# Idle accumulator banks for the gates, relu fused into the residual, fewer masks in the chains, squares on ScalarE: a graph network on one core

## The chip, the core and the metric

The kernel runs on one core of a Trainium2 chip. The metric is device time in microseconds of one execution. The kernel before takes 737.91 us, the median of three runs (737.57 to 739.96); the execution in its profile spans 734.9 us. PE, DVE, ACT, POOL and SP below are TensorE, VectorE, ScalarE, GpSimd and SyncE, as in the profile.

## The reference

x has 3327 nodes with 64 features, adj is 3327 x 3327, sparse in content (about one entry in 200 is not zero) but stored dense. Four layers follow each other, each with a layernorm ahead of it; the sums with x are the residuals.

```python
h = relu(layernorm(x))            # layer 0: two gated convolutions
for W, wih, whh in layer0:
    m = adj @ (h @ W)
    r, z, n = gru_gates(m @ wih.T, h @ whh.T)
    h = relu((1 - z) * n + z * h)
x = x + h

h = relu(layernorm(x))            # layer 1: the ranked layer
mask = adj != 0
rank = cumsum(mask, axis=1); deg = rank[:, -1:]
k = minimum(deg, 100); pos = rank - (deg - k)
w = mask * where(pos > 0, 0.5 ** (k - pos), 0)
x = x + w @ (h @ W) + b

h = relu(layernorm(x))            # layer 2: three hops
for W, b in layer2:
    h = ((adj * adj) @ h) @ W.T + b
x = x + h

g = h = relu(layernorm(x))        # layer 3: two hops
for W in layer3:
    h = tanh(concat([adj @ h, h], 1) @ W)
x = x + h
```

## The kernel before, in words

**Passes and chunks.** Eight times adj is multiplied with features: passes k = 0 and 1 for layer 0, k = 2 for the ranked layer, 3 to 5 for the squared hops, 6 and 7 for the last two (KIND, line 70). The destination nodes lie in four chunks of 384, 384, 384 and 512 columns, twice over (two halves s; CH, line 51), and the chunks in two groups, 0 and 1, 2 and 3 (GROUPS). adj [...]is streamed from memory in every pass: 26 tiles of 128 source nodes for each group, each 128 x 2 x 768 or 896 numbers of 32 bits (load, L325), into 20 slots. `alone` and `joint` (L555 to L620) write out the order of the units (pass, chunk, tile), such that a tile once loaded serves two passes; `run` (L622) loads 60 units ahead, prepares up to 44 units ahead, and expands EXPAND = 3 units ahead of the matmuls of `propagate` (L517), which sum into a PSUM bank per chunk.

**The engines' order** is the order in which this program issues the instructions; nothing rearranges it later. Each engine takes its own in that order.

**Chains.** When a chunk's sum is complete, a chain of work begins (`after_0` to `after_7`), for the chunk's new features: a gated cell (`gru`, L737: evacuation of the sum L704 and L705, four gates L748, sigmoids L753, DVE work L757 to L768, relu L773 in the second cell), transposes (through `mm`, L229), the residual (L728), a layernorm (L713 to L724, of which L720, a power, runs on GpSimd), and for the ranked layer the features as a sum of three bf16 terms (`in_three`, L791 and L793). A chain is a generator; each `yield` gives microseconds of PE work after which it may go on, and `spend` (L294) lets chains go on as matmuls are issued. A unit that needs features which a chain has not yet made runs this chain to its end (L508).

**Banks.** [...]four for sums of `propagate`, four for everything else. `take` (L238) gives an idle one; with either=True, which only the ranked weights use, it may also be an idle bank of the sums.

**The ranked pass.** w isn't computed from a cumulative sum along all columns, but by tiles: a mask of each tile (adj != 0, bf16, two `piece`s of L383 on DVE), whose last row is filled by a DMA of GpSimd (L388) with the number of entries in later tiles (counted by L453 during pass 0). A matmul with a triangular matrix (`tri`, through `mm`, L229) gives the exponents, and an eviction with a relu turns them into int16, which is the bit pattern of the bf16 weight (`e`): L431 on DVE or L433 on ACT, by the rule in L430. `propagate` multiplies e with the three terms of the features. Pieces wait in a queue (`pieces`); L645 to L648 issue some of them per unit, and `mask_pieces(t=t)` (L424) issues what is still missing of a tile when the tile is expanded. A tile is called "own" of a group where its sources lie among the group's destinations. In group 0 the own tiles come last in pass 2, right after group 0's chains of pass 1, so DVE and ACT do chains and weights there at the same time.

**The rest of what is touched.** `square` (L358) squares a tile of adj for the squared passes, two of three on ACT (L360), one of three on DVE (L362). `last_sources` (L469) fetches the last row of every tile for a group and makes its weights (L481, L485, L487); it is begun at 70 us of PE work for group 0, 230 for group 1 (L914).

The lines below are those of the kernel before.

Of the kernel before, what the change touches and what calls it, by code (L numbers as in the profile page):

```python
# [12 lines left out]
AF = mybir.ActivationFunctionType  # L13
ALU = mybir.AluOpType
# [37 lines left out]
NC = len(CH)  # L52
CWM = 512
GROUPS = [(0, 1), (2, 3)]
# [39 lines left out]
def kernel(  # L94
# [9 lines left out]
    nc = tc.nc  # L104
# [116 lines left out]
    def width(c):  # L221
        return blocks(c) * P
# [12 lines left out]

    released = [0] * 8

    def take(sums=False, either=False):  # L238

        pool = idle_sums if sums else idle_temps  # L240
        if either and idle_sums and (not pool or released[idle_sums[0]] < released[pool[0]]):
            pool = idle_sums
        for c in list(tasks):
            if not pool and c not in running:
                advance(c)
        i = pool.popleft()
        return i, banks[i]
# [9 lines left out]
    def flat(t):  # L257
        return t.rearrange("p b s d -> p b (s d)")
# [4 lines left out]
    def xchunk(c):  # L263
        return xs[:, CH[c][0]:CH[c][1]]
# [5 lines left out]
    tasks = {}  # L270
# [10 lines left out]
    def begin(c, task):  # L281
        finish(c)
        tasks[c] = [task, 0.0]
        advance(c)

    def finish(c):
        while c in tasks:
            advance(c)

    def later_task(us, task):  # L290
        yield us
        yield from task
# [12 lines left out]
    sums = {}  # L305
# [50 lines left out]
                spare.append(self.at)  # L356

    def square(sq, v, turn):  # L358
        if turn % 3:
            nc.scalar.activation(sq, v, AF.Square)  # L360
        else:
            nc.vector.tensor_tensor(sq, v, v, ALU.mult)  # L362
# [31 lines left out]
    def mask_pieces(n=0, t=None):  # L394

        while pieces and (n > 0 or any(u is t for u, _, _ in pieces)):
            _, half, piece = pieces.popleft()
            piece(half)
            n -= 1

    def expand(k, c, t):

        if k == COUNT:
            return None
        w = width(c)
        if t is SPECIAL:
            g = c // 2
            w0 = (CH[c][0] - CH[GROUPS[g][0]][0]) * P
            finish(NC + 1 + g)
            return lastw[g][:, w0:w0 + w].bitcast(BF16)  # L410
        if KIND[k] == PLAIN or (KIND[k] == SQUARED and t.in_place):
            return t.view(c)
        if KIND[k] == SQUARED:
            room = Mask(t.w)
            wide = room.view.rearrange("p s w -> p (s w)").bitcast(F32)[:, :2 * w].rearrange("p (s w) -> p s w", s=2)
            square(wide, t.view(c), t.q + c)
            squared[k, c, t] = room
            return wide
        wide = work.tile([P, 2, CWM], I16, name="e", bufs=4)[:, :, :w]

        mask_pieces(t=t)  # L424
        for s in range(2):
            i, ps = take(either=True)
            mm(ps[:, :w], tri, t.mask.view[:, s, t.cols(c)])
            own = chunk_of(t.q % NB) in GROUPS[t.g]
            busy = any((k - 1, ch) in sums for ch in GROUPS[t.g])
            if s and (own if t.g == 0 and (own or busy) else c == GROUPS[t.g][1]):  # L430
                nc.vector.tensor_scalar(wide[:, s], ps[:, :w], BITS, 0.0, op0=ALU.add, op1=ALU.max)  # L431
            else:
                nc.scalar.activation(wide[:, s], ps[:, :w], AF.Relu, bias=bitsb)  # L433
            give(i)
        spend(STREAM_US * w / CWM * 0.5)
        if c == GROUPS[t.g][1]:
            t.mask.free()
        return wide.bitcast(BF16)

    ranks_left = set(sources_of(*GROUPS[0]))  # L440
    counts = {}
    squared = {}

    def count(t, first, last):


        mask_pieces(t=t)
        for c in GROUPS[t.g]:
            w = width(c)
            if first:  # L450
                counts[c] = take()
            for s in range(2):
                nc.tensor.matmul(counts[c][1][s * D:(s + 1) * D, :w], behind[:, NQ - 1 - t.q:NQ - 1 - t.q + D],  # L453
                                 t.mask.view[:, s, t.cols(c)], start=first, stop=last)
            spend(STREAM_US * w / CWM * 0.25)
            if last:
                begin(("count", c), count_done(c))
        t.mask.free()
# [163 lines left out]
    def run():  # L622
        total = {}
        for k, c, t in units:
            total[k, c] = total.get((k, c), 0) + 1
        done = {}
        loaded, prepared, expanded = 0, 0, deque()
        for i, (k, c, t) in enumerate(units):
            while loaded < len(units) and loaded < i + LOAD:
                u = units[loaded][2]  # L630
                if u is not SPECIAL and u.slot is None:
                    if len(dead) <= RESERVE and loaded > i + EXPAND:
                        break
                    u.load()
                loaded += 1
            while prepared < loaded and prepared < i + PREPARE[KIND[units[prepared][0]] if units[prepared][0] != COUNT
                                                               else COUNT]:
                if prepared > i + PREPARE[PLAIN] and not spare and len(dead) <= RESERVE + 1:
                    break
                prepare(*units[prepared])  # L640
                prepared += 1
            while len(expanded) < min(EXPAND + 1, len(units) - i):
                assert prepared > i + len(expanded)
                expanded.append(expand(*units[i + len(expanded)]))
            if k != 2:  # L645
                mask_pieces(1 + len(pieces) // 6)
            elif not (c in GROUPS[0] and (t is SPECIAL or chunk_of(t.q % NB) in GROUPS[0])):
                mask_pieces(1)  # L648
            n = done[k, c] = done.get((k, c), 0) + 1
            propagate(k, c, t, expanded.popleft(), n == 1, n == total[k, c])  # L650

# [72 lines left out]
        nc.vector.scalar_tensor_tensor(groups(h), xc[:, :n], 0.0, st[:, 3, :n, None].to_broadcast([P, n, D]),  # L724
                                       op0=ALU.max, op1=ALU.mult)

    def residual(v, c):
        nc.vector.tensor_tensor(flat(xchunk(c)), flat(xchunk(c)), v[1], ALU.add)  # L728
        give(v[0])

    def add_row(c, i):
# [5 lines left out]
    def gru(acc, c, bi, bh, cell, pace=1.0):  # L737

        w = width(c)
        evacuate_stacked(acc, c)  # L740
        yield 0.8 * pace
        at = dead.popleft()
        r, z, d = (slots[at].rearrange("p s w -> p (s w)")[:, i * CWM:i * CWM + w] for i in range(3))

        def gate(g):
            i, ps = take()
            for s in range(2):
                nc.tensor.matmul(ps[upper(1 - s), :w], cells[:, cell, s, g, :], both[c][:, s], start=True, stop=True)  # L748
            return i, ps

        for g, v in enumerate((r, z)):
            i, ps = gate(g)
            nc.scalar.activation(v, ps[:, :w], AF.Sigmoid, bias=bsum[:, cell, g:g + 1])  # L753
            give(i)
        pn = gate(2), gate(3)
        yield 1.0 * pace
        nc.vector.scalar_tensor_tensor(r, pn[0][1][:, :w], bcol[:, bh + 2:bh + 3], r, op0=ALU.add, op1=ALU.mult)  # L757
        nc.vector.tensor_tensor(r, r, pn[1][1][:, :w], ALU.add)
        for i, _ in pn:
            give(i)  # L760
        yield 1.0 * pace
        nc.scalar.activation(r, r, AF.Tanh, bias=bcol[:, bi + 2:bi + 3])
        yield 0.8 * pace
        for s in range(2):
            u = upper(1 - s)
            nc.vector.tensor_tensor(d[u], both[c][u, s], r[u], ALU.subtract)
        nc.vector.tensor_tensor(d, d, z, ALU.mult)
        nc.vector.tensor_tensor(d, d, r, ALU.add)  # L768
        if cell == 0:
            nc.scalar.activation(both[c][upper(1), 0], d[upper(1)], AF.Relu)  # L770
            nc.vector.tensor_scalar(both[c][upper(0), 1], d[upper(0)], 0.0, None, op0=ALU.max)
        else:
            nc.scalar.activation(d, d, AF.Relu)  # L773
        yield 2.8 * pace
        return at, d

# [43 lines left out]
    def after_1(c, acc):  # L820
        pace = 1.0 if c in GROUPS[0] else 1.2
        at, h2T = yield from gru(acc, c, BI2, BH2, 1, pace)
        v = transpose_to_nodes(h2T, c)
        dead.append(at)
        yield 0.8 * pace
        residual(v, c)
        yk = nodes(c)
        yield from layernorm_relu(yk, c, TWO27, 1.2 * pace)
        y[2][c] = yield from in_three(yk, c)
        yield 6.0  # L830
        add_row(c, 3)
# [79 lines left out]
            begin(c, before_0(c))  # L911
    begin(NC, more_constants())
    begin(NC + 1, later_task(70.0, last_sources(0)))
    begin(NC + 2, later_task(230.0, last_sources(1)))  # L914
    run()
    for c in list(tasks):
        finish(c)
# [39 lines left out]
```

## Time and profile before

| what | value |
| --- | --- |
| median of three runs | 737.91 us |
| profiled span | 734.9 us |
| sums of the plain and squared passes, PE L517 f32 | 536.0 us busy, 2912 records |
| sums of the ranked pass, PE L517 bf16 | 72.9 us, 624 records |
| masks by tri, PE L229 bf16 (temp and sum banks) | 67.0 us, 416 records |
| mask pieces, DVE L383 | 112.5 us, 208 instructions |
| squares, ACT L360 and DVE L362 | 113.7 us in 138, 69.4 us in 70 |
| evictions to e from temp banks, ACT L433 and DVE L431 | 68.8 us in 123, 23.5 us in 37 |
| evictions to e from sum banks, ACT L433 and DVE L431 | 13.6 us in 24, 13.7 us in 24 |
| rows of totals, issued by POOL (L388) | 52 |
| power of the layernorm, POOL L720 | 27.0 us in 16 |
| relu of the second cell, ACT L773 | 2.2 us in 4 |

A row of the page gives line, engine, operation, output and inputs by their names in the program, the count, the busy time and the mean of one. "Idle before" is how long the engine stood ahead of such an instruction, and behind the arrow is what ended that. In the timelines of a single engine, a row is a run of like instructions from its start, with its length, and in brackets the idle time ahead of it. In a table of stretches each engine has its busy time and its count, in the order PE, weight load, DVE, ACT, POOL; then come the clock granted to PE and the share and rate of the DMA.

### The profile page before, as it was taken

Reading aid. Unit: us, or ns where it says so; the run is one execution under the profiler, and the core shown is the slowest. Engines: PE = TensorE matmul, PEld = TensorE weight load, DVE = VectorE, ACT = ScalarE, POOL = GpSimd, SP = SyncE. Lnnn points to the kernel's source line nnn. Section 1 sums busy time; section 2 is a strip of 40 time slices with the busy share of each in tenths; the row PEclk is TensorE's granted clock in tenths of the full one; section 3 lists DMA queues with packets and bytes.
Section 4 is the critical chain, followed back from the end, with each engine's and each line's share of the span. In section 5 each row is a group of like instructions: output and inputs, shape, how many; then the busy total and the mean of one; then the engine's idle time right before and its main releaser. Section 6 shows DMA issues by size and latency. Waiting matters only on the chain. (4 is left out here: it accounts for less than half of the span.)

```text
span 734.9 us, 12499 instructions
## 1 busy us (share of the span) xinstructions
PE 694.7 (95%) x5112; PEld 347.6 (47%) x5112; DVE 340.1 (46%) x599; ACT 244.6 (33%) x383; POOL 72.6 (10%) x105
## 2 busy tenths in 40 slices
PE   5988999899999898989899999999999999999997
PEld 2543566344546685545344444334344454344443
DVE  6656736434997978758764114321252520000101
ACT  0103100212037767768848213730044601000101
POOL 4100000001290502112200000000110000000000
PEclk9999999999999999999999999999999999999999
DMA  9999996189587365571799749953987399916991
GB/s 340 401 357 405 405 392 213 44 323 364 179 288 280 105 219 186 183 283 45 276 351 383 263 145 408 406 230 109 393 298 251 126 396 405 401 39 238 399 403 38
DMA packets 68964, 201.54 MB, mean 274 GB/s; under 512 B 7388, under 2 KB 8644, under 8 KB 68908
## 3 DMA queue, kind: packets, MB, share of 16 engines
q1 hardware_dynamic: 66156, 199.70, 73.2%
q8 instruction: 40, 0.66, 0.4%
q10 hardware_dynamic: 576, 0.85, 0.3%
q0 software_dynamic: 2176, 0.20, 0.2%
q14 instruction: 16, 0.13, 0.0%
HBM read 199.68 MB, written 0.85 MB: 273 GB/s over the span
## 5 line engine op out<-in xcount | busy, mean ns | idle before, releaser
L517 PE MATMUL sum<-adj,y 128*64 128x384 f32 (+1 forms) x2912 | 536.0, 516 | 17.8 <-DMA adj<-in_adjT 13.5
L517 PEld LDWEIGHTS sum<-adj,y 128*64 128x64 f32 x2912 | 218.4, 138 | 274.0 <-issue 230.3
L360 ACT ACTIVATE adj<-adj 128x768 f32<-128x768 f32 (+1 forms) x138 | 113.7, 891 | 57.7 <-PE sum L517 36.6
L383 DVE TENSOR_SCALAR adj<-adj 128x768 bf16<-128x768 f32 (+3 forms) x208 | 112.5, 593 | 33.5 <-PE temp L453 29.5
L362 DVE TENSOR_TENSOR adj<-adj 128x768 f32<-128x768 f32 (+1 forms) x70 | 69.4, 1022 | 57.1 <-DMA adj<-in_adjT 32.6
L433 ACT ACTIVATE e<-temp,bitsb 128x384 int16<-128x384 f32 (+1 forms) x123 | 68.8, 600 | 24.2 <-PE temp L229 18.4
L517 PE MATMUL sum<-e,adj 128*64 128x384 bf16 (+1 forms) x624 | 72.9, 339 | 0.0
L705 DVE COPY both<-sum 64x384 f32<-64x384 f32 (+1 forms) x16 | 9.5, 594 | 130.5 <-ACT both L704 130.5
L704 ACT COPY both<-sum 64x384 f32<-64x384 f32 (+1 forms) x16 | 8.0, 499 | 149.4 <-PE sum L517 149.4
L229 PE MATMUL temp<-adj,tri 128*64 128x384 bf16 (+1 forms) x320 | 49.6, 346 | 7.9 <-DMA adj<-totals 2.5
L720 POOL TENSOR_TENSOR st<-st,mhalf 128x6 f32<-128x6 f32 (+1 forms) x16 | 27.0, 1688 | 301.1 <-DVE st L719 292.6
L517 PEld LDWEIGHTS <-adj 128*64 128x64 bf16 x624 | 41.3, 110 | 17.2 <-issue 5.3
L388 POOL DMA_DIRECT2D adj<-totals x52 | 31.4, 606 | 134.6 <-DVE adj L768 74.7
L229 PEld LDWEIGHTS <-tri 128*64 128x64 bf16 x416 | 28.6, 111 | 29.2 <-issue 14.7
L431 DVE TENSOR_SCALAR e<-temp 128x512 int16<-128x512 f32 (+1 forms) x37 | 23.5, 634 | 20.5 <-PE temp L229 11.4
L748 PE MATMUL temp<-both,cells 128*64 128x384 f32 (+1 forms) x128 | 27.4, 521 | 4.1 <-DVE adj L757 2.2
L658 DVE COPY t<-sum 128x384 f32<-128x384 f32 x8 | 4.4, 556 | 54.3 <-PE sum L517 54.3
L453 PE MATMUL temp<-adj,behind 128*64 128x384 bf16 x208 | 28.6, 339 | 0.3 <-DVE adj L383 0.2
L656 ACT COPY t<-sum 128x384 f32<-128x384 f32 (+1 forms) x8 | 4.3, 533 | 67.0 <-PE sum L517 67.0
L700 ACT COPY both<-temp 64x384 f32<-64x384 f32 (+1 forms) x16 | 8.0, 502 | 55.5 <-PE temp L694 55.4
L453 PEld LDWEIGHTS <-behind 128*64 128x64 bf16 x208 | 16.2, 110 | 16.2 <-issue 14.4
L229 PE MATMUL sum<-adj,tri 128*64 128x384 bf16 (+1 forms) x96 | 17.4, 335 | 2.4 <-DVE e L431 2.4
(83 smaller groups left out, 293.5 us busy)
## 6 DMA issues: line engine op xcount, KB each, us to landing
adj<-in_adjT SPq DMA_DIRECT2D x130, 768.0 KB, 7.7
adj<-in_adjT SPq DMA_DIRECT2D x104, 896.0 KB, 11.6
xs<-in_x SPq DMA_DIRECT2D x1, 640.0 KB
out<-xs ACTq DMA_DIRECT2D x3, 192.0 KB, 1.9
adj<-totals POOLq DMA_DIRECT2D x26, 3.0 KB, 4.6
adj<-totals POOLq DMA_DIRECT2D x26, 3.5 KB, 2.2
folds<-in_weights SPq DMA_DIRECT2D x4, 64.0 KB, 11.8
out<-xs ACTq DMA_DIRECT2D x1, 256.0 KB
```

The source lines that it names most:

```text
L229: nc.tensor.matmul(out[hs], lhsT[:, hs], rhs, start=start, stop=stop)
L360: nc.scalar.activation(sq, v, AF.Square)
L362: nc.vector.tensor_tensor(sq, v, v, ALU.mult)
L383: nc.vector.tensor_scalar(t.mask.view[:rows, half], t.view()[:rows, half], 0.0, None, op0=ALU.not_equal)
L388: nc.gpsimd.dma_start(out=t.mask.view[P - 1:P], in_=totals[t.g][t.q:t.q + D + 1:D, :])
L431: nc.vector.tensor_scalar(wide[:, s], ps[:, :w], BITS, 0.0, op0=ALU.add, op1=ALU.max)
L433: nc.scalar.activation(wide[:, s], ps[:, :w], AF.Relu, bias=bitsb)
L453: nc.tensor.matmul(counts[c][1][s * D:(s + 1) * D, :w], behind[:, NQ - 1 - t.q:NQ - 1 - t.q + D], t.mask.view[:, s, t.cols(c)], start=firs ...
L517: nc.tensor.matmul(acc[h * D:(h + 1) * D, :w], yq[h], rhs[h], start=first and n == 0, stop=last and n == len(terms) - 1)
L705: nc.vector.tensor_copy(both[c][upper(1), 1], acc[1][upper(1), :width(c)])
L720: nc.gpsimd.tensor_tensor(st[:, 3, :n], st[:, 2, :n], mhalf[:, :n], ALU.pow)
L748: nc.tensor.matmul(ps[upper(1 - s), :w], cells[:, cell, s, g, :], both[c][:, s], start=True, stop=True)
```

## The change

Gates, transposes and the other temporary results may take an idle bank of the sums (`take`, either=True by default), except for the counts. The relu after the second cell is no instruction of its own any more: the residual takes max(v, 0) and adds in one DVE instruction. In pass 2 the mask pieces that were issued one per unit ahead of need are no longer issued while group 0 runs and any chunk has a chain under way. While a ranked sum of group 1 is open, all squares go to ScalarE, not two of three. The rule of L430 gives the second half of a weight to DVE more often in the units that are not own. The last sources of group 1 are begun at 175 us of PE work instead of 230.

```diff
--- before.py
+++ after.py
@@ -235,8 +235,10 @@
 
     released = [0] * 8
 
-    def take(sums=False, either=False):
-
+    def take(sums=False, either=True):
+
+
+        either = either and not sums
         pool = idle_sums if sums else idle_temps
         if either and idle_sums and (not pool or released[idle_sums[0]] < released[pool[0]]):
             pool = idle_sums
@@ -356,7 +358,7 @@
                 spare.append(self.at)
 
     def square(sq, v, turn):
-        if turn % 3:
+        if turn % 3 or any((2, c) in sums for c in GROUPS[1]):
             nc.scalar.activation(sq, v, AF.Square)
         else:
             nc.vector.tensor_tensor(sq, v, v, ALU.mult)
@@ -423,11 +425,11 @@
 
         mask_pieces(t=t)
         for s in range(2):
-            i, ps = take(either=True)
+            i, ps = take()
             mm(ps[:, :w], tri, t.mask.view[:, s, t.cols(c)])
             own = chunk_of(t.q % NB) in GROUPS[t.g]
             busy = any((k - 1, ch) in sums for ch in GROUPS[t.g])
-            if s and (own if t.g == 0 and (own or busy) else c == GROUPS[t.g][1]):
+            if s and (own if t.g == 0 and (own or busy) else not own or c == GROUPS[t.g][1]):
                 nc.vector.tensor_scalar(wide[:, s], ps[:, :w], BITS, 0.0, op0=ALU.add, op1=ALU.max)
             else:
                 nc.scalar.activation(wide[:, s], ps[:, :w], AF.Relu, bias=bitsb)
@@ -448,7 +450,7 @@
         for c in GROUPS[t.g]:
             w = width(c)
             if first:
-                counts[c] = take()
+                counts[c] = take(either=False)
             for s in range(2):
                 nc.tensor.matmul(counts[c][1][s * D:(s + 1) * D, :w], behind[:, NQ - 1 - t.q:NQ - 1 - t.q + D],
                                  t.mask.view[:, s, t.cols(c)], start=first, stop=last)
@@ -645,7 +647,8 @@
             if k != 2:
                 mask_pieces(1 + len(pieces) // 6)
             elif not (c in GROUPS[0] and (t is SPECIAL or chunk_of(t.q % NB) in GROUPS[0])):
-                mask_pieces(1)
+                if c in GROUPS[1] or not any(ch in tasks for ch in range(NC)):
+                    mask_pieces(1)
             n = done[k, c] = done.get((k, c), 0) + 1
             propagate(k, c, t, expanded.popleft(), n == 1, n == total[k, c])
 
@@ -724,8 +727,11 @@
         nc.vector.scalar_tensor_tensor(groups(h), xc[:, :n], 0.0, st[:, 3, :n, None].to_broadcast([P, n, D]),
                                        op0=ALU.max, op1=ALU.mult)
 
-    def residual(v, c):
-        nc.vector.tensor_tensor(flat(xchunk(c)), flat(xchunk(c)), v[1], ALU.add)
+    def residual(v, c, relu=False):
+        if relu:
+            nc.vector.scalar_tensor_tensor(flat(xchunk(c)), v[1], 0.0, flat(xchunk(c)), op0=ALU.max, op1=ALU.add)
+        else:
+            nc.vector.tensor_tensor(flat(xchunk(c)), flat(xchunk(c)), v[1], ALU.add)
         give(v[0])
 
     def add_row(c, i):
@@ -769,8 +775,6 @@
         if cell == 0:
             nc.scalar.activation(both[c][upper(1), 0], d[upper(1)], AF.Relu)
             nc.vector.tensor_scalar(both[c][upper(0), 1], d[upper(0)], 0.0, None, op0=ALU.max)
-        else:
-            nc.scalar.activation(d, d, AF.Relu)
         yield 2.8 * pace
         return at, d
 
@@ -823,7 +827,7 @@
         v = transpose_to_nodes(h2T, c)
         dead.append(at)
         yield 0.8 * pace
-        residual(v, c)
+        residual(v, c, relu=True)
         yk = nodes(c)
         yield from layernorm_relu(yk, c, TWO27, 1.2 * pace)
         y[2][c] = yield from in_three(yk, c)
@@ -911,7 +915,7 @@
             begin(c, before_0(c))
     begin(NC, more_constants())
     begin(NC + 1, later_task(70.0, last_sources(0)))
-    begin(NC + 2, later_task(230.0, last_sources(1)))
+    begin(NC + 2, later_task(175.0, last_sources(1)))
     run()
     for c in list(tasks):
         finish(c)
```

## The prediction, on record before the changed kernel ran

> **What bounds the kernel now.** I read the page first, then PE's waits, then busy time by stretch, then the timelines around the longest waits.
>
> The page's first part:
>
> ```profile
> PE 694.7 (95%) x5112; PEld 347.6 (47%) x5112; DVE 340.1 (46%) x599; ACT 244.6 (33%) x383; POOL 72.6 (10%) x105
> ```
>
> PE is busy for 694.7 of 734.9 us. The change removes no matmul, so it can win only PE's idle time, or the part of it that other engines cause. Who caused it stands in PE's waits (total, times, longest):
>
> ```profile
> PE sum L517 <- DVE y L724: 3.1, 1, 3.1
> PE temp L229 <- DMA adj<-totals: 2.5, 1, 2.5
> PE sum L229 <- DVE e L431: 2.4, 3, 1.4
> PE temp L748 <- DVE adj L757: 2.2, 1, 2.2
> PE temp L229 <- DVE adj L383: 2.0, 3, 1.6
> PE temp L748 <- ACT both L704: 1.9, 1, 1.9
> ```
>
> The longest wait of all, 13.5 us for tiles of adj, lies mostly ahead of 60 us and is not touched. What is touched lies in the ranked phase (208 to 360 us). Busy time of PE, PEld, DVE, ACT, POOL, then clock and DMA:
>
> ```profile
> 236.00:256.00 20.00, 15.49 (x190) 12.07 (x191) 19.59 (x44) 15.02 (x31) 8.56 (x12) 1.00 0.38 126
> ...
> 272.00:292.00 20.00, 17.59 (x200) 13.38 (x198) 15.85 (x31) 13.69 (x26) 3.82 (x4) 1.00 0.65 226
> ...
> 318.00:330.00 12.00, 9.54 (x62) 4.09 (x60) 6.52 (x11) 6.49 (x10) 2.16 (x4) 0.86 0.72 273
> ...
> 346.00:361.00 15.00, 11.87 (x120) 6.62 (x118) 11.85 (x20) 11.62 (x16) 1.93 (x1) 1.00 0.74 263
> ```
>
> In 236 to 256 VectorE is full (19.59 of 20), so it is the bound there, not PE. In 318 to 330 PE is short by 2.5 us and ran at clock 0.86. The two single waits behind the last two rows, from PE's timeline:
>
> ```profile
> 323.74 0.52 PE L229 MATMUL temp<-adj,tri 128*64 128x384 bf16 x4 [2.46 <-DMA adj<-totals]
> ...
> 360.23 15.26 PE L517 MATMUL sum<-adj,y 128*64 128x384 f32 x84 [3.13 <-DVE y L724]
> ```
>
> The first waits for a row of totals (L388) in a mask, the second for a layernorm. GpSimd issues those rows, and its timeline shows what they queue behind:
>
> ```profile
> 278.63 1.35 POOL L720 TENSOR_TENSOR st<-st,mhalf 128x6 f32<-128x6 f32 x1 [20.57 <-DVE st L719]
> 286.10 1.32 POOL L720 TENSOR_TENSOR st<-st,mhalf 128x6 f32<-128x6 f32 x1 [6.12 <-DVE st L719]
> 287.37 1.20 POOL L388 DMA_DIRECT2D adj<-totals  x2
> ```
>
> VectorE's timeline gives the price of a layernorm's first half:
>
> ```profile
> 274.21 0.56 DVE L431 TENSOR_SCALAR e<-sum 128x384 int16<-128x384 f32 x1 [0.91 <-PE sum L229]
> 274.69 0.54 DVE L728 TENSOR_TENSOR xs<-xs,temp 128x384 f32<-128x384 f32 x1
> ...
> 276.53 0.68 DVE L431 TENSOR_SCALAR e<-sum 128x512 int16<-128x512 f32 x1
> ```
>
> From the start of one e to the start of what follows L715 it is 276.53 - 274.21 = 2.32 us.
>
> **What the Trainium skill says.** "Perfetto Trace Analysis", section Tensor Engine Instruction: PE can pull only weight loads ahead, VectorE, ScalarE and GpSimd run strictly in order; so a matmul that waits holds all matmuls behind it, and a row holds behind an L720. The trace agrees: at 287.37 two rows start as L720 ends. "DMA: Bandwidth & Descriptors", section Anatomy of one DMA: about 2 us fixed for a DMA issued by GpSimd. The trace has a median of 2.2 us for these rows of 3.5 KB, and 1.6 to 5.6 over all 52 of L388; I use the trace's. "TensorE: Matmul & The Clock Gate", Part 1: after an idle window of about 3.4 us the clock halves until a busy one. Here the 2.46 us wait was followed by clock 0.86 over 12 us, that is 12 x 0.14 = 1.7 us lost.
>
> **The change part by part.** In the built change the order of PE's matmuls is the same one; only their banks, and the order on VectorE, ScalarE and GpSimd, differ.
>
> Banks for gates: the 2.16 us wait at 68.77 (L748 <- L757, a bank) goes. The gates then wait for both1, written at 66.35 + 0.56 = 66.91, and PE got there at 66.60: gain 1.8. At 143.29 the gates need both3, which stays, but the later gates no longer wait for L167 to empty a bank: the 16 matmuls took 4.40 us to the next one, and from L705's end (143.96) the 14 or 15 left of them at about 0.215 each would need 3.15, to 147.1 instead of 147.69: gain 0.6.
>
> Relu in the residual: 4 ScalarE ops (L773, 3 x 0.52 + 0.63) vanish, and with them PE's 0.40 wait at 190.97. On VectorE L728 becomes a scalar_tensor_tensor; from bank to SBUF its price lies between L728's 0.55 and L757's 0.62, at most 4 x 0.07 = 0.3, in chains where other work fills the gaps. Gain 0.4.
>
> No masks in group 0's chains: between the last L768 and the last L793 VectorE's order loses 12 pieces L383 of 896 columns (1.15 per pair, 6.9 us) and gains 8 evictions L431, which moved from ScalarE (0.47 each in a row, 3.8): 19.6 us become 16.5. PE's own work there: undisturbed, six matmuls with e follow each other every 0.815 us (257.34 to 258.16); from 240.56 to 255.72 13 such steps took 15.2 instead of 10.6, and 235.12 to 240.56 lost another 1.5. So PE lost 6.1, just what VectorE has over it (19.6 - 13.6 = 6.0). With 16.5 the excess is 2.9, of which three units of look-ahead (EXPAND, 2.4 us) can hide a part. I take 2.1 lost: gain 4.0 (3 to 5.5).
>
> What it adds: group 1's masks. Before, rows and pieces of six tiles were done by 255. In the changed order none is: the first pieces stand behind the residual and first half of the layernorm of chunk 0, and the next rows behind an L720. The stretch, from the end of chunk 0's L229 on bd (273.60) to the seventh mask's first matmuls (291.03): 8 pairs on tri of 384 (0.33), 6 of 512 (0.43), 11 sums of 384 (0.49), 5 of 512 (0.65), one bd (0.66) make 14.5 us; before took 17.4, so lost 2.9. By hand, with t = 0 at bd's end, an eviction starting 0.1 after a matmul's modelled end:
> first tile: e at 0.61, pieces done at 3.55 and 4.08; PE is there at 1.31: idle 2.65.
> second: L719 ends at 7.45, L720 at 8.95, the row is issued then and lands 2.2 later, 11.1; PE is there at 5.69: idle 5.45.
> third: its pieces wait for the evictions of the second: idle 2.0. Fourth: 0.85.
> fifth: behind chunk 1's L728 to L715 (2.32 again): 2.6.
> sixth: behind chunk 1's L720, as the second: 3.15. Seventh: 0.3.
> Sum 17.0; with rows at 1.6 instead of 2.2 it is 15.8, at 5.6 it is 23.8. Against 2.9: loss 14.1. An idle of 5.45 us is longer than the 2.46 that halved the clock, so I add 1.0 for that (0 to 1.7): 15.1. Queued behind each waiting tri matmul are all later sums, and so the evictions and pieces that need them. One late half mask in group 0 costs another 0.5 (PE reaches it 0.49 after its predecessor, the piece is ready after 1.1).
>
> The wait at 323.74: its row now takes a half slot that PE frees 0.9 us earlier. Before, the row took 5.4 (318.30 to 323.7); if again, the wait is 1.5; at the median it is gone. I take 1.5 won of 2.46, and 1.2 of the clock's 1.7: gain 2.7 (0 to 4.2).
>
> Squares to ScalarE: 10 of 70 L362 go. Two of 1.2 us each stood between L715 and L717 ahead of the 360.23 wait: 2.35 us less, of which PE gets 2.3. ScalarE takes the three of that place in a gap of 1.98 us ahead of L656; in 292 to 318 it does 10 us of squares and loses 22 evictions over the phase, VectorE the reverse, both beside a full PE (25.80 of 26): nothing. The last sources at 175: L481 and L485 (0.6 + 1.1) and L487 (1.0) move to 256 to 272, where VectorE has 3.8 us free and PE look-ahead: nothing.
>
> Sum: 1.8 + 0.6 + 0.4 + 4.0 + 2.7 + 2.3 = 11.8 won; 15.1 + 0.5 = 15.6 lost; 3.8 net, rounded to 3.6 since the terms are no better: 737.9 + 3.6 = 741.5.
>
> **The rivals.** Faster: rows land in 1.6 us, the clock stays up (15.8 - 2.9 = 12.9 lost), and the gains reach their ends (1.8 + 0.6 + 0.4 + 5.5 + 4.2 + 2.6 = 15.1): 735.7 or a little less, 735. For it: VectorE's 19.59 of 20 shows how much the masks hurt there. Against: the serial chain in group 1 holds whatever the rows do. Chance 0.26.
> No change: gains of 12 to 13 against 12.9: 738. Chance 0.22.
> Much slower: rows take 5 us, as the one at 318.30, and the clock falls twice: 741.5 + 2 x 2.8 + 0.7 = 748. For it: that row; against: the median. Chance 0.12. The forecast itself 0.40.
>
> **How the numbers follow.** Slower has 0.40 + 0.12 = 0.52. The range goes from just under the faster rival to the slow one: 734.5 to 748.
>
> **What would show it.** PE waits of 2 to 5 us at L229 for adj<-totals and L383, some 33 us of stretch after chunk 0's bd; the waits at 68.77 and 190.97 gone; VectorE under 18 us in the chains; the 3.1 us wait for L724 under 1. Wrong if the first masks of group 1 come without such waits: then it is 10 us faster than I say.

## The result and the profile after

The changed kernel takes 748.74 us (median of six runs, 747.13 to 750.17), the kernel before beside it 738.62 us: ratio 1.0133, 95% interval 1.0112 to 1.0154. It is slower by 10.1 us (1.3%); the forecast was 741.5, and the range ended at 748.0. The profile of before shows an execution of 736.59 us, 2 us under this median, that of after one of 748.45 us: the two traces differ by 11.8 us, the medians by 10.1.

In the changed kernel the same instructions stand some lines lower: L519 is the sums (L517 before), L385 the pieces (L383), L390 the rows of totals (L388), L433 and L435 the evictions on DVE and ACT (L431, L433), L723 the power (L720), L727 the layernorm's end (L724), L754 the gates (L748), L763 and L772 to L774 DVE work of the cell (L757, L766 to L768).

The page's first part, and PE's waits (total, times, longest):

```profile
PE 699.1 (94%) x5112; PEld 361.7 (48%) x5112; DVE 341.6 (46%) x611; ACT 241.7 (32%) x367; POOL 71.4 (10%) x105
```

```profile
PE temp L229 <- DMA adj<-totals: 10.6, 3, 4.6
PE sum L519 <- DVE y L727: 8.7, 2, 8.1
PE temp L229 <- DVE adj L385: 5.3, 6, 2.1
PE temp L229 <- DVE e L433: 4.5, 5, 1.4
...
PE temp L754 <- ACT both L707: 1.9, 1, 1.9
```

The gates' wait for a bank is gone. Of the 8.7 us for L727, 8.1 lie ahead of the first matmul, where the kernel before waits 8.5 us for tiles of adj; of its 3.1 us wait for L724 only 0.6 is left. New is most of the 10.6 us for rows of totals (2.5 before) and of the 5.3 us for pieces (2.0 before). The waits for evictions on VectorE are hardly longer in total: 4.5 us, before 3.6, which are the 2.4 us that the prediction shows and this line of before:

```profile
PE temp L229 <- DVE e L431: 1.2, 3, 0.6
```

How far the changed kernel is behind the kernel before, in the two traces, follows from the start of the same matmul in each:

| place (us before) | before | after | after - before | forecast for the stretch up to here |
| --- | --- | --- | --- | --- |
| first matmul | 8.52 | 8.12 | -0.40 | 0 |
| 191.5, first layer done | 191.49 | 187.98 | -3.51 | -2.8 (banks, relu) |
| 231.2, group 0's chains | 231.20 | 228.69 | -2.51 | 0 |
| 261.1, chains done | 261.08 | 258.91 | -2.17 | -4.0 |
| 290.3, seventh mask of group 1 | 290.34 | 308.65 | +18.31 | +15.6 |
| 330.4, after the wait at 323.74 | 330.36 | 345.66 | +15.30 | -2.7 |
| 367.8, after the wait at 360.23 | 367.80 | 379.64 | +11.84 | -2.3 |

After that nothing changes: +11.8 to the end. Three of the forecast's terms are there in about the size it gave or somewhat more: banks and relu, the wait at 323.74, the squares. Two aren't: the chains won nothing, and group 1's masks cost 20.5 us (+18.31 less -2.17) instead of 15.6. Between 191 and 231 us, where nothing was forecast, 1.0 us was lost.

Busy time in that stretch of group 1, from the end of chunk 0's bd to the seventh mask, before and after (time, PE, PEld, DVE, ACT, POOL, clock, DMA):

```profile
273.60:290.34 16.74, 14.51 (x165) 10.98 (x162) 13.34 (x27) 11.56 (x21) 3.82 (x4) 1.00 0.69 239
```

```profile
272.14:308.65 36.51, 21.29 (x164) 11.76 (x162) 22.42 (x44) 11.07 (x17) 6.93 (x9) 0.72 0.41 139
```

PE's timeline of after, and GpSimd's, in this stretch:

```profile
275.75 0.35 PE L229 MATMUL temp<-adj,tri 128*64 128x384 bf16 x2 [2.12 <-DVE adj L385]
...
277.16 0.69 PE L229 MATMUL sum<-adj,tri 128*64 128x512 bf16 x2
277.58 0.69 PE L229 MATMUL temp<-adj,tri 128*64 128x512 bf16 x2
...
283.75 0.53 PE L229 MATMUL temp<-adj,tri 128*64 128x384 bf16 x2 [4.51 <-DMA adj<-totals]
...
295.27 0.35 PE L229 MATMUL temp<-adj,tri 128*64 128x384 bf16 x2 [1.53 <-DVE adj L385]
296.40 0.35 PE L229 MATMUL temp<-adj,tri 128*64 128x384 bf16 x2 [0.78 <-DVE adj L385]
...
297.29 0.64 PE L229 MATMUL sum<-adj,tri 128*64 128x512 bf16 x2
297.72 0.64 PE L229 MATMUL temp<-adj,tri 128*64 128x512 bf16 x2
...
303.91 0.53 PE L229 MATMUL temp<-adj,tri 128*64 128x384 bf16 x2 [4.59 <-DMA adj<-totals]
...
309.62 0.41 PE L229 MATMUL temp<-adj,tri 128*64 128x512 bf16 x2
309.84 0.41 PE L229 MATMUL sum<-adj,tri 128*64 128x512 bf16 x2
```

```profile
280.49 1.59 POOL L723 TENSOR_TENSOR st<-st,mhalf 128x6 f32<-128x6 f32 x1 [24.42 <-DVE st L722]
282.05 2.21 POOL L390 DMA_DIRECT2D adj<-totals  x4
297.76 1.35 POOL L723 TENSOR_TENSOR st<-st,mhalf 128x6 f32<-128x6 f32 x1 [13.50 <-DVE st L722]
299.08 1.30 POOL L390 DMA_DIRECT2D adj<-totals  x2
```

The serial chain is the one that was worked out: a row is issued as L723 ends, at 282.05 and 299.08, and PE's long waits end 1.7 and 4.8 us later. All waits of the stretch, nine of them, are 15.2 us (forecast 17.0). But PE was also slow: the two pairs of 512 columns at 277.16 and 277.58 are 0.42 apart, those at 297.29 and 297.72 0.43, where the same step takes 0.22 at full clock (309.62 to 309.84). Stretch less work less waits is 36.5 - 14.5 - 15.2 = 6.8 us, and PE's busy time is longer by as much for the same matmuls (21.29 for 14.51). With a granted clock of 0.72 in the stretch this is put down to the halved clock; the forecast had 1.0.

### The profile page after: what moved, and what is told of

The parts are those of the page before. It is cut to its first block, busy times and chain, and to the rows that moved or that the text cites. A ratio compares the mean times of both kernels' runs of the same rounds, so it can differ in the third digit from the quotient of the medians.

```text
span 746.7 us, 12487 instructions
## 1 busy us (share of the span) xinstructions
PE 699.1 (94%) x5112; PEld 361.7 (48%) x5112; DVE 341.6 (46%) x611; ACT 241.7 (32%) x367; POOL 71.4 (10%) x105
## 5 line engine op out<-in xcount | busy, mean ns | idle before, releaser
L519 PE MATMUL sum<-adj,y 128*64 128x384 f32 (+1 forms) x2912 | 536.7, 515 | 13.9 <-DVE y L727 8.7
L519 PEld LDWEIGHTS sum<-adj,y 128*64 128x64 f32 x2912 | 228.3, 138 | 260.4 <-issue 212.5
L362 ACT ACTIVATE adj<-adj 128x768 f32<-128x768 f32 (+1 forms) x148 | 122.6, 891 | 58.2 <-PE sum L519 36.6
L385 DVE TENSOR_SCALAR adj<-adj 128x768 bf16<-128x768 f32 (+3 forms) x208 | 112.4, 592 | 32.8 <-PE temp L455 28.8
L364 DVE TENSOR_TENSOR adj<-adj 128x768 f32<-128x768 f32 (+1 forms) x60 | 58.6, 1011 | 57.3 <-DMA adj<-in_adjT 28.6
L519 PE MATMUL sum<-e,adj 128*64 128x384 bf16 (+1 forms) x624 | 75.9, 350 | 0.5 <-ACT e L435 0.5
L229 PE MATMUL temp<-adj,tri 128*64 128x384 bf16 (+1 forms) x332 | 54.2, 354 | 20.8 <-DMA adj<-totals 10.6
L435 ACT ACTIVATE e<-temp,bitsb 128x384 int16<-128x384 f32 (+1 forms) x105 | 60.5, 602 | 39.6 <-PE temp L229 28.9
L723 POOL TENSOR_TENSOR st<-st,mhalf 128x6 f32<-128x6 f32 (+1 forms) x16 | 26.1, 1630 | 328.5 <-DVE st L722 320.0
L519 PEld LDWEIGHTS <-adj 128*64 128x64 bf16 x624 | 41.8, 113 | 20.7 <-issue 8.5
L433 DVE TENSOR_SCALAR e<-temp 128x384 int16<-128x384 f32 (+1 forms) x61 | 36.6, 607 | 25.1 <-PE temp L229 11.3
L390 POOL DMA_DIRECT2D adj<-totals x52 | 30.7, 592 | 125.3 <-DVE adj L774 74.2
L703 ACT COPY both<-temp 64x384 f32<-64x384 f32 (+1 forms) x12 | 5.9, 492 | 48.6 <-PE temp L697 48.5
L754 PE MATMUL temp<-both,cells 128*64 128x384 f32 (+1 forms) x80 | 19.9, 522 | 1.9 <-ACT both L707 1.9
L433 DVE TENSOR_SCALAR e<-sum 128x384 int16<-128x384 f32 (+1 forms) x22 | 12.4, 565 | 14.6 <-PE sum L229 13.9
## 6 DMA issues: line engine op xcount, KB each, us to landing
adj<-in_adjT SPq DMA_DIRECT2D x104, 896.0 KB, 10.9
```

Of the source, the lines that this page charges most:

```text
L229: nc.tensor.matmul(out[hs], lhsT[:, hs], rhs, start=start, stop=stop)
L385: nc.vector.tensor_scalar(t.mask.view[:rows, half], t.view()[:rows, half], 0.0, None, op0=ALU.not_equal)
L390: nc.gpsimd.dma_start(out=t.mask.view[P - 1:P], in_=totals[t.g][t.q:t.q + D + 1:D, :])
L519: nc.tensor.matmul(acc[h * D:(h + 1) * D, :w], yq[h], rhs[h], start=first and n == 0, stop=last and n == len(terms) - 1)
L723: nc.gpsimd.tensor_tensor(st[:, 3, :n], st[:, 2, :n], mhalf[:, :n], ALU.pow)
```

## The experiments

Every run was timed beside the kernel before, which had 737.8 to 738.6 us in these comparisons. Theory A: the masks without a lead set the loss. Theory B: the evictions that the new rule of L430 gives to VectorE do.

### Masks, evictions, and both

The mask rule taken back in the changed kernel (**masks_undone**), or put alone into the kernel before (**masks_only**):

```diff
             elif not (c in GROUPS[0] and (t is SPECIAL or chunk_of(t.q % NB) in GROUPS[0])):
-                if c in GROUPS[1] or not any(ch in tasks for ch in range(NC)):
-                    mask_pieces(1)
+                mask_pieces(1)
```

> The changed kernel, with mask pieces issued one per unit in group 0's chains again; all other parts of the change stay. Theory A (group 1's masks have no lead, and that costs 20 us): the stretch after chunk 0's bd falls from 36.5 us to about 17.5, but VectorE gets 6.9 us of pieces on top of its 17.4 in group 0's chains, which costs PE up to 5: 733.5, between 730 and 737. Theory B (the evictions moved to VectorE by the rule of L430 stand in each other's way, and the masks matter little): 742 or more.

> The kernel before, with only the rule that issues no mask pieces while group 0 runs and a chain is under way. Theory A: group 1's masks lose their lead, 12 us of waits and 6 us of a halved clock, against 3 to 6 us won in group 0's chains where VectorE loses 6.9 us of work: 753, between 749 and 757. Theory B: the masks alone cost less than 5: 743 or less.

masks_undone: 736.23 us, ratio 0.9969 (0.9953 to 0.9985), in the range of theory A. masks_only: 748.33 us, 1.0143 (1.0120 to 1.0166), 5 us under the value expected, just under its range, and still as slow as the whole change. The mask rule costs 9.9 us alone (738.48 us beside it) and 12.5 us with the rest of the change.

The rule of L430 taken back (**evictions_undone**), alone (**evictions_only**), and taken back together with the mask rule (**both_undone**):

```diff
-            if s and (own if t.g == 0 and (own or busy) else not own or c == GROUPS[t.g][1]):
+            if s and (own if t.g == 0 and (own or busy) else c == GROUPS[t.g][1]):
```

> The changed kernel with the old rule of L430 for which evictions go to VectorE. Theory A: the wait for masks stays, and VectorE's order in group 0's chains loses 8 evictions (3.8 us), which gives back the forecast gain there: 745.5, between 743 and 748. Theory B: back to about 738 or less.

> The kernel before with only the new rule of L430. If the evictions moved to VectorE cost by themselves (VectorE is full in group 0's chains with the mask pieces, and ScalarE isn't): 738 + 5.5 = 743.5, between 741 and 746. If they cost only together with other parts: 738.

> The changed kernel with both the mask rule and the rule of L430 as before; banks, relu, squares and last sources stay changed. Theory A with evictions as a second cost of their own (about 6 us, as the run with the old rule of L430 showed): 736.2 - 6 = 730.4, between 728 and 733. If evictions cost only where the masks are missing: 736, as with the mask rule alone undone.

evictions_undone: 742.29 us, 1.0066 (1.0040 to 1.0092), 6.4 less than the changed kernel and just below the range expected. evictions_only: 747.93 us, 1.0131 (1.0097 to 1.0165), above its range; expected was 743.5. both_undone: 731.40 us, 0.9899 (0.9869 to 0.9929), as expected.

So with the remaining edits in place:

| us | pieces also in the chains | no pieces in the chains |
| --- | --- | --- |
| old rule of L430 | 731.4 | 742.3 |
| new rule of L430 | 736.2 | 748.7 |

The mask rule costs 10.9 or 12.5, the eviction rule 4.8 or 6.4, the remaining edits win 6.8 (738.2 to 731.4). Both theories are right, each for a part: each rule costs much the same with and without the other. On the way from the kernel before to the changed one the steps are -6.8 + 10.9 + 6.4 = +10.5.

Where the eviction rule costs shows in busy time over group 0's chains, between the same two matmuls: the kernel before, after, and evictions_undone:

```profile
231.20:261.08 29.88, 25.31 (x324) 20.11 (x322) 28.17 (x60) 22.07 (x45) 10.95 (x16) 1.00 0.53 181
```

```profile
228.69:258.91 30.22, 25.48 (x324) 20.29 (x322) 28.64 (x61) 17.33 (x33) 8.12 (x12) 1.00 0.45 154
```

```profile
228.81:253.84 25.03, 24.27 (x325) 21.11 (x323) 22.09 (x48) 21.33 (x43) 8.10 (x12) 1.00 0.54 182
```

With the old rule VectorE loses the 12 pieces against before (60 to 48), and the stretch shrinks by 4.9 us. The new rule adds 13 instructions (48 to 61). Nine are evictions; four are work of the first cell (L772 to L774), which the other two kernels have done before the stretch begins. VectorE is busy for 28.64 of 30.22 us again, while ScalarE falls to 17.33: the room that the pieces left was filled, and PE got nothing. Why the cell is late shows in VectorE's timeline, first after, then evictions_undone:

```profile
228.05 0.56 DVE L433 TENSOR_SCALAR e<-sum 128x384 int16<-128x384 f32 x1 [2.63 <-PE sum L229]
228.64 1.12 DVE L772 TENSOR_TENSOR adj<-both,adj 64x384 f32<-64x384 f32 x2
```

```profile
224.99 0.56 DVE L433 TENSOR_SCALAR e<-sum 128x384 int16<-128x384 f32 x1
225.58 1.12 DVE L772 TENSOR_TENSOR adj<-both,adj 64x384 f32<-64x384 f32 x2
```

An eviction that the new rule gives to VectorE stands ahead of the cell in its order, and VectorE stood for 2.63 us until PE had written the result that it empties. masks_undone and evictions_only, with the new rule too, stand 2.17 and 2.16 us at the same place; both_undone and masks_only, with the old one, don't.

In the four kernels of the table this stretch takes 30.0 and 25.0 us with the old rule, 35.7 and 30.2 with the new one: the pieces cost 5.0 or 5.5 us there, the new rule 5.2 or 5.7. Alone, without room, the rule makes it 35.97 us long (evictions_only, 29.88 before), with VectorE at 34.53. The rest of what it costs the changed kernel lies in group 1, 36.51 against 34.67 in evictions_undone; what it does there stays open.

### What makes the masks of group 1 slow

**clock_filled** puts matmuls that nobody reads into PE's long waits, so that the clock stays up:

```diff
+    group_1 = []
...
         mask_pieces(t=t)
+        if t.g == 1 and c == GROUPS[1][0]:
+            n = len(group_1) + 1
+            group_1.append(t)
+            if n in (1, 2, 5, 6):
+                i, ps = take()
+                for _ in range(4 if n in (2, 6) else 2):
+                    mm(ps, ident, cells.rearrange("p c h g d -> p (c h g d)")[:, :CWM])
+                give(i)
```

> The changed kernel with matmuls that nobody reads (512 columns f32, 2, 4, 2 and 4 pairs of 0.86 us) ahead of the four masks of group 1 that PE waited for longest (2.1, 4.5, 1.5 and 4.6 us). They lie in idle time. Theory A with the clock (6.8 us of the 36.5 are matmuls at half clock): the clock stays near 1.0 and the time falls by 3 to 6, to 744.5. If the slow stretch is only waits, nothing is won: 748.5 to 750.

747.94 us, 1.0126 (1.0099 to 1.0154): no gain that can be told from none. The clock was full in the stretch, whose rows of busy time are:

```profile
272.00:290.00 18.00, 14.19 (x126) 7.46 (x122) 11.96 (x25) 5.10 (x10) 3.77 (x5) 1.00 0.52 186
290.00:309.00 19.00, 15.22 (x116) 7.39 (x118) 12.90 (x25) 8.85 (x13) 3.67 (x5) 1.00 0.31 99
```

The stretch became 3.8 us shorter (36.51 to 32.75), not 6.8: with work of 14.5 us again, PE's waits and the matmuls in them take 18.2 us, where the waits alone were 15.2. A faster PE waits longer for the same chain. And 2.9 us were given back later: the wait for a row that is 1.52 us at 340.74 in after was 1.97 at 338.49 here, and the clock fell in its neighbourhood (0.91 over 326 to 346, where after has 1.00 over 330 to 350). That the clock costs time is shown in the stretch; in the whole time it is not.

**rows_early** takes L720 out of the rows' way: GpSimd issues the row when the mask's room is taken, not with its first piece.

```diff
         def piece(half):
             nc.vector.tensor_scalar(t.mask.view[:rows, half], t.view()[:rows, half], 0.0, None, op0=ALU.not_equal)
-            if half == 0 and kind == RANKED:
-                for ch in GROUPS[t.g]:
-                    finish(("count", ch))
-                nc.gpsimd.dma_start(out=t.mask.view[P - 1:P], in_=totals[t.g][t.q:t.q + D + 1:D, :])
             if half == 1:
                 t.used()
+
+        if kind == RANKED:
+            for ch in GROUPS[t.g]:
+                finish(("count", ch))
+            nc.gpsimd.dma_start(out=t.mask.view[P - 1:P], in_=totals[t.g][t.q:t.q + D + 1:D, :])
```

> The changed kernel, but GpSimd issues the row of totals when the mask's room is taken, not together with the mask's first piece; the pieces stay where they are. Theory A1 (of group 1's serial chain, the part behind L720 and the row's landing costs most): the two waits of 4.5 and 4.6 us for rows shrink to the end of the pieces, 2.3 and 4.2 us sooner, and so does the 1.5 us wait at 340: 741.5, between 739 and 745. Theory A2 (VectorE's pieces in line with the layernorm set the pace, rows only come last by chance): 747 or more.

741.98 us, 1.0050 (1.0034 to 1.0066), as theory A1 had it. PE's waits in its stretch are now for pieces:

```profile
276.79 0.35 PE L229 MATMUL temp<-adj,tri 128*64 128x384 bf16 x2 [2.11 <-DVE adj L385]
...
282.19 0.35 PE L229 MATMUL temp<-adj,tri 128*64 128x384 bf16 x2 [1.68 <-DVE adj L385]
```

The stretch is 28.06 us instead of 36.51. Rows that queue behind the power thus make 8.5 us of the 19.8 by which the stretch grew, with the clock that their waits cost; the waits that are left are for pieces.

### The other edits

The squares (L358) and the banks (L238), each taken back in the changed kernel:

```diff
-        if turn % 3 or any((2, c) in sums for c in GROUPS[1]):
+        if turn % 3:
```

```diff
-    def take(sums=False, either=True):
+    def take(sums=False, either=False):
...
-            i, ps = take()
+            i, ps = take(either=True)
             mm(ps[:, :w], tri, t.mask.view[:, s, t.cols(c)])
```

> The changed kernel with one square of three on VectorE again in the ranked phase. If the squares between L715 and L717 were what held the layernorm of 360.23, that wait comes back: 751.2, between 750 and 753. If the wait went by another part of the change (banks, earlier residual), nothing changes: 748.7.

> The changed kernel, with sum banks for the ranked weights only, as before. If the gates' wait for a bank at 68.77 and the later gates at 143 us were worth 1.8 and 0.6 us: the two come back and no more, 748.7 + 2.4 = 751, between 749.5 and 752.5. If the banks were worth nothing: 748.7.

squares_undone: 753.07 us, 1.0190 (1.0165 to 1.0216). The 3.1 us wait for the layernorm is back, with this line of PE's timeline (its first 18 matmuls), and the trace is 4.7 us behind that of the changed kernel from there on. Of these 2.6 are the wait (3.12 us for 0.56) and 1.6 slower matmuls behind it: the 84 that follow took 16.91 us, in after and before 15.26:

```profile
375.12 5.20 PE L519 MATMUL sum<-adj,y 128*64 128x384 f32 x18 [3.12 <-DVE y L727]
```

banks_undone: 752.07 us, 1.0186 (1.0165 to 1.0208). It is 2.3 us behind the changed kernel by 150 us, with the wait for a bank in PE's timeline again, and 1.0 more around 220 us:

```profile
68.22 3.05 PE L754 MATMUL temp<-both,cells 128*64 128x384 f32 x16 [2.16 <-DVE adj L763]
```

The relu and the last sources were not tried alone. In every trace with the relu in the residual the lead grows by 0.6 us at the transposes of 191 us, where L773's wait of 0.40 was; no run shows the part of the last sources.

### The lead regained

If pieces are bad in the chains and missing in group 1, there is a place between: 247 to 266.4 us, where evictions_undone has VectorE free for 4.1 of 19.4 us. **lead_regained** keeps the old rule of L430 and issues pieces in all units of the ranked pass of group 0, but not while a chain is under way. **lead_and_rows** adds the early rows. **lead_balanced** instead adds that, while pieces are issued there, every other tile's eviction that VectorE would have goes to ScalarE:

```diff
-            elif not (c in GROUPS[0] and (t is SPECIAL or chunk_of(t.q % NB) in GROUPS[0])):
-                if c in GROUPS[1] or not any(ch in tasks for ch in range(NC)):
-                    mask_pieces(1)
+            elif c in GROUPS[1] or not any(ch in tasks for ch in range(NC)):
+                mask_pieces(1)
...
-            if s and (own if t.g == 0 and (own or busy) else not own or c == GROUPS[t.g][1]):
+            if s and (own if t.g == 0 and (own or busy) else c == GROUPS[t.g][1]) and not (
+                    t.g == 0 and pieces and t.q % 2 and not any(ch in tasks for ch in range(NC))):
```

> The changed kernel with the old rule of L430 and one mask piece per unit in group 0's own units too, as long as no chain is under way: no pieces lie in the chains, but twelve are issued after them and ahead of group 1. Theory A: the 34.7 us stretch of the run with the old rule of L430 falls to about 18, and the pieces (13 x 0.58 = 7.5 us against 4.1 us that VectorE has free there) cost up to 3.5: 729, between 726 and 733, faster than both kernels. If the lead isn't what counts: 740 or more.

> The run before this one and the early rows of totals together. Theory A1: with lead the rows matter only at the wait near 340 (1.3 us and its clock): 727, between 724 and 731. If rows issued early hold back L720 in GpSimd's order: slower than the run before this one.

> The kernel that has its lead regained, with every other eviction of group 0's own units on ScalarE while mask pieces are issued there (between the chains and group 1). VectorE was full there (8.00 and 7.51 us of 8) and ScalarE not (5.67 and 3.05), and PE lost 3.6 us: if VectorE's work is what costs them, 2 are won: 726.5, between 724 and 728. If not: 728.5.

lead_regained: 728.54 us, 0.9870 (0.9838 to 0.9902). lead_and_rows: 728.62 us, 0.9856 (0.9830 to 0.9883), no different: with a lead, early rows bring nothing that can be seen. lead_balanced: 725.70 us, 0.9833 (0.9798 to 0.9868), its interval overlapping that of lead_regained, so that a gain over it is not shown by the times. All three beat both kernels. Of lead_balanced, group 0's chains, and group 1's stretch:

```profile
228.79:253.84 25.05, 24.28 (x325) 21.14 (x323) 22.12 (x48) 21.36 (x43) 10.23 (x17) 1.00 0.54 184
266.69:283.91 17.22, 14.53 (x164) 11.13 (x161) 12.80 (x27) 13.24 (x23) 3.75 (x4) 1.00 0.83 292
```

The chains are as short as without pieces (25.05), and the stretch as short as with them (17.22 against 16.74 before). Between the two, from the end of the first to that of chunk 0's bd, it takes 12.85 us, lead_regained 16.10 and the kernel before 12.52. With every other eviction on ScalarE, the pieces cost PE next to nothing there in this trace.

## Why the prediction was wrong

The prediction had the mask rule and the eviction rule together at 15.6 - 4.0 = 11.6 us lost, and the other edits at 7.8 us won. The runs show 17.3 lost (731.4 to 748.7) and 6.8 won. By its steps:

- **Banks 1.8 + 0.6, relu 0.4.** Right: the trace won 3.1 us up to 191 us, beyond its 0.4 us earlier start. banks_undone confirms 2.3 of it; it also shows 1.0 near 220 us that the forecast didn't have.
- **No masks in group 0's chains, 4.0 won.** This is the first step that failed: 0.3 us was lost. In the window in which it counted, from the last L768 to the last L793, the count was right, 12 pieces out and 8 evictions in. But VectorE's time there fell from 19.6 to 17.4 us (235.80 to 253.22 in after), not to 16.5, and PE won only 1.0 us (235.12 to 255.72 in before). Ahead of the window the step counted nothing, and PE lost 1.3 us (231.20 to 235.12): two more evictions are on VectorE there, and it stood 2.63 us for one of them. Without the new rule the same step would have been right, and rather low: 4.9 us.
- **The eviction rule, charged within that step.** Its term was too small. Without the evictions the same count leaves VectorE 16.5 - 3.8 = 12.7 us, less than PE's 13.6, and all of the 6.1 us that PE lost would have been won; with 4.0 won, the rule was charged 2.1, part of it hidden by look-ahead. In this stretch it cost 5.2 us (30.22 for 25.03), in the whole time 4.8 to 6.4, and 9.7 alone. The nine evictions at 0.47 us are 4.2 of that, so little can have been hidden; that the rest is the standing ahead of the cell fits, but no run separates it.
- **Group 1's masks just in time, 14.1 lost, +1.0 clock.** The mechanism was right, and its waits too (15.2 us measured, 17.0 worked out). The term for the clock is the second that failed: 6.8 us measured in the changed kernel for 1.0. The prediction charged one wait, of 5.45 us, as "The Trainium skill", page "TensorE: Matmul & The Clock Gate", Part 1, has the clock halve after an idle window of about 3.4 us. But its own trace had a lower clock after 2.46 us, and its sum has three more waits of 2.6 to 3.15 us. The trace of after shows the half pace at 277.16, after a wait of 2.12 us and a short burst of work, and again at 297.29, after waits of only 1.53 and 0.78 us. So waits well under 3.4 us brought the half pace here, and the length of a single wait doesn't decide it: the matmuls after the 3.13 us at 360.23 in before ran at full pace, those after the 3.12 us in squares_undone took 1.6 us longer. Of the 19.8 us by which the stretch grew, the mask rule makes 36.51 - 18.84 = 17.7 (masks_undone), and 34.67 - 18.87 = 15.8 with the old rule of L430 (evictions_undone, both_undone). Some 2.1 us more than before are there with the pieces too (18.84 and 18.87 for 16.74); why stays open.
- **Wait at 323.74, 2.7 won.** The sum is right, 3.0, but by luck in part. The wait fell by 0.9 us, to 1.52 at 340.74, where 1.5 won was taken; the matmuls behind it, now at full pace, won 1.7 where 1.2 was taken; 0.4 was won earlier. Which part of the change won it stays open: masks_only and evictions_only don't have it, and the runs that take back the squares, the banks, the masks or the evictions all keep it. That leaves the last sources or the relu, which were not tried alone, or several parts together.
- **Squares, 2.3 won.** Right: the wait fell by 2.6 us, from 3.13 to 0.56; the other 0.9 of the table's 3.5 were won ahead of it. Taken back they cost more, 4.3 us (squares_undone), with the clock that fell behind the wait.

By the traces the chains were 4.3 us worse than forecast and group 1's stretch 4.9. Either alone, added to 741.5, would have stayed within the range; the two together, less what other steps won beyond the forecast, put the time 0.7 us beyond it. The rival "much slower", 748, came out near the time, but for another cause: it had the rows at 5 us each and one more fall of the clock, and only one of the two rows after L723 took that long.

## What to carry to other kernels

When a change both takes work off a full engine and puts other work on it, count both over the whole stretch in which that engine is full, not over the window in which the wait was seen, and ask of each piece of work that is put there what it waits for: what stands behind it in that engine's order waits too. Work that runs ahead of need is best moved to where its engine has room, not dropped until needed: in the traces the same pieces cost 16 us just in time, 5 us amid the chains, and next to nothing between the two once the evictions were shared out. And edits that come together should each be costed alone: here two were bad for 17 us, the others together good for 7.

## What was not expected

- Two rows of the same 3.5 KB, both issued by GpSimd right after a power, took 1.7 and 4.8 us until PE could go on (282.05 to 283.75, 299.08 to 303.91).
- Matmuls ran at half pace after waits of 1 to 2 us that follow each other, and once at full pace after one of 3.1 us; over the 36.5 us of the stretch the granted clock was 0.72.
- Keeping the clock at 1.00 with filler matmuls won 3.8 us of that stretch, and nothing that can be told from none in the whole time (747.9 against 748.7).
